# Decoder layer on one Trainium2 core: the router's columns after the second Gram matrix, the expert ranks in larger pieces, the last layer norm by 128 tokens

## The chip, the core and the metric

The kernel runs on one core of a Trainium2 chip. The core has TensorE (PE in the profile, with its weight loads as PEld), VectorE (DVE), ScalarE (ACT), GpSimd (POOL) and SyncE (SP), which here issues all the DMAs. Each engine works through its own instructions in order, and waits on semaphores for the others. The metric is the device time of one execution in microseconds (us).

## The reference

The reference is one decoder layer, on 16 sequences (B) of 512 tokens (S) with 256 channels (C), in float32. There are three sublayers, each followed by a residual sum and a layer norm without gain:

```python
x = layernorm(x + self_attention(x))           # linear: prod over 2 k of (k^T v), no softmax; inner norm, Wo
x = layernorm(x + cross_attention(x, context)) # 16 heads of 64, 64 context tokens a sequence, Wq, Wkv, Wout
x = layernorm(x + mixture_of_experts(x))       # 8 experts, 256 -> 1024 -> 256, relu

# mixture of experts: each expert serves the first `capacity` tokens, in order, with weight > 0
capacity = ceil(b * s / e * 1.0)               # 16*512/8 = 1024
w = softmax(x @ router_w.T + router_b)
out = relu(tokens @ experts_inter[e]) @ experts_out[e] * w
```

Softmax weights are practically never zero. So the expert sublayer serves the first 1024 tokens, that is batches 0 and 1, unless some weight underflows; which tokens are served is nevertheless computed from the weights.

## The kernel before

**Parts.** The linear self-attention is computed from one Gram matrix x^T x of each batch (`gram`, L544: two halves of matmuls, L549 and L554, into one PSUM bank `ps_g`; copies into `g` and `u`; a transpose `ps_gt`, L567). The cross attention first makes keys of the whole context: `context_keys` (L444) transposes the context and the weights (`ps_t`, L233), computes blocks of 128x512 (`ps_kv`, L436, two matmuls each, called kv1, kv2, ... here), copies each into a tile `st` (a pool of two buffers, by DVE or ACT in turn, L188 and L186) and stores it to `k_dram` (L464). The main part of the program then goes through the 16 batches: self-attention, cross attention (`ps_sim` L808, softmax, the transpose into `pT` L798, `ps_x` L828), layer norm, routing. The experts work on the head, batches 0 and 1 (`HEAD_B`, 1024 tokens), in four groups of `TB` = 256 tokens an expert: eight blocks f of `ps_h` (L932, two matmuls each), each with its relu into a tile `hT` by DVE (even f, L940) or ACT (odd f, L938), then `ps_e` (L949), 8 matmuls for each of the two 128-token tiles, and the weighted sum into `x2_head` (L956) on DVE. After the last expert the head is normalised and stored (L960 to L964). The rest of the batches are stored before that, after their own norm (L866); a loop at the end of the program repeats the experts for `n_i` of them, and `n_i` is 0 with these inputs.

**Layer norm.** `normalized` (L252) takes the moments by BN statistics on DVE (L249, L250), makes the reciprocal deviation by Ln and Exp on ACT (L261, L262), yields, then makes the offset `off` on DVE (L265) and applies both on ACT, one instruction for each 128 tokens (L267).

**Router columns.** `router_columns` (L371) turns the router's weights into columns that are appended to other weight matrices, so that router logits come out of later matmuls as 8 more columns (264 = 256 + 8). It has three DVE operations on 8 partitions (L374 to L376), two small transposes (`ps_rw`, L379) and one copy (L380). Its result is read by `router_weights` (L403, about 64 us) and later.

**Ranks.** `ranks` (L869) decides from all the weights which tokens each expert serves: a comparison (L885), two matmuls for sums over tokens (`ps_tot`, L889, and `ps_in`, L891) with their copies (L892, L893), a running sum over 64 token tiles in six doubling rounds (L897, L898), then the ranks, the selected weights `w_sel` and the number of loop rounds `n_i` (L901 to L912). All but the two matmuls is on DVE. It runs after the routing of the last batch.

**Order.** The order of the instructions is written down when the program is built. Six generators, the streams (`grams`, `context`, `self`, `cross`, `routing`, `experts`), issue their instructions piece by piece. `weave` always lets one go on to its next `yield`. A model of engine times (class `Model`, L28) estimates when each piece would end. `yield WAIT` makes a stream ready again only at the modelled end of its last piece, `yield 0.6` in 0.6 us, a plain `yield` at once; among the ready streams that with the smallest planned time (`plan(at, span, total)`) goes next. `beside` starts another stream with its parent's planned time. `in_order` then binds the instructions of PE, DVE, ACT and POOL to this order, so an instruction that waits holds up everything behind it on its engine, also where that is of another stream. SP issues its DMAs in order as well.

Of the kernel before, what the change touches and what calls it, by code (L numbers as in the profile page):

```python
# [9 lines left out]
FP = mybir.dt.float32  # L10
# [8 lines left out]
P = 128  # L19
# [5 lines left out]
WAIT = "wait"  # L25
# [91 lines left out]
def decoder_layer(  # L117
# [25 lines left out]
    nc = tc.nc  # L143

    B, S, C = x.shape
    J = context.shape[1]
    NT = S // P
# [8 lines left out]
    E, _, FF = w_inter.shape  # L156
# [5 lines left out]
    CX = C + E  # L162
    TB = 256
# [52 lines left out]
    x2_head = const.tile([P, HEAD_B, NT, CX], FP, tag="x2_head", name="x2_head")  # L216
# [35 lines left out]
    def normalized(dst, src, NT=NT, mm=None):  # L252


        rstd = small.tile([P, NT], FP, tag="rstd", name="rstd")
        if mm is None:
            mm = moments(NT)
            for t in range(NT):
                moment(mm, t, src(t))
        mv = mm[1]  # L260
        nc.scalar.activation(rstd, mv[:, :, 1], AF.Ln, bias=eps)  # L261
        nc.scalar.activation(rstd, rstd, AF.Exp, scale=-0.5)  # L262
        yield WAIT
        off = small.tile([P, NT], FP, tag="off", name="off")
        nc.vector.scalar_tensor_tensor(off, mv[:, :, 0], -1.0, rstd, ALU.mult, ALU.mult)  # L265
        for t in range(NT):
            nc.scalar.activation(  # L267
                dst[:, t, :], src(t), AF.Identity, bias=off[:, t:t + 1], scale=rstd[:, t:t + 1]
            )


    with ExitStack() as att:
# [17 lines left out]
        wk1 = pool(att, "wk1", 1)  # L290
# [30 lines left out]
        def key_weights():  # L321
# [14 lines left out]
            out=hm, in_=hm, pattern=[[0, NC], [-HD, P // HD], [0, HD]], compare_op=ALU.is_ge,  # L336
# [3 lines left out]
            out=hm, in_=hm, pattern=[[0, NC], [HD, P // HD], [0, HD]], compare_op=ALU.is_ge,  # L340
# [528 lines left out]
        def ranks():  # L869

            place = wk1.tile([P, 7, NTT, E], FP, tag="kq", name="ranks")
            consts = place[:, 6].rearrange("p t e -> p (t e)")
            ones, before = consts[:, :P], consts[:, P:2 * P]
            nc.gpsimd.memset(ones, 1.0)

            nc.gpsimd.affine_select(
                out=before, in_=ones, pattern=[[1, P]], compare_op=ALU.is_gt, fill=0.0,
                base=0, channel_multiplier=-1,  # L880
            )
            pos, tot, cum, nxt, start, rank = (place[:, i] for i in range(6))


            nc.vector.tensor_single_scalar(pos, w_all, FLT_MIN, ALU.is_ge)  # L885
            posf = pos.rearrange("p t e -> p (t e)")
            yield
            ps_tot = bank("ps_tot")
            nc.tensor.matmul(ps_tot, ones, posf, start=True, stop=True)  # L889
            ps_in = bank("ps_in")  # L890
            nc.tensor.matmul(ps_in, before, posf, start=True, stop=True)  # L891
            nc.vector.tensor_copy(tot.rearrange("p t e -> p (t e)"), ps_tot)  # L892
            nc.vector.tensor_copy(rank.rearrange("p t e -> p (t e)"), ps_in)  # L893
            yield
            src, s = tot, 1
            while s < NTT:
                nc.vector.tensor_copy(nxt[:, :s, :], src[:, :s, :])  # L897
                nc.vector.tensor_add(nxt[:, s:, :], src[:, s:, :], src[:, :NTT - s, :])  # L898
                src, nxt, s = nxt, (cum if src is tot else src), s * 2
                yield  # L900
            nc.vector.tensor_sub(start, src, tot)  # L901
            nc.vector.tensor_add(rank, rank, start)
            nc.vector.scalar_tensor_tensor(w_sel, rank, float(CAP), w_all, ALU.is_lt, ALU.mult)
            NB = B - HEAD_B
            least = small.tile([P, NB], FP, tag="least", name="least")
            nc.vector.tensor_reduce(
                least, start.rearrange("p (b t) e -> p b t e", t=NT)[:, HEAD_B:, 0, :], AX.X, ALU.min
            )
            nc.vector.tensor_single_scalar(least, least, float(CAP), ALU.is_lt)
            n_f = small.tile([P, 1], FP, tag="n_f", name="n_f")  # L910
            nc.vector.tensor_reduce(n_f, least, AX.X, ALU.add)
            nc.vector.tensor_copy(n_i, n_f)  # L912
            yield

        def experts():

            wi = wo_ = None
            yield from until(lambda: 0 in head_T and made(head_T[0]))  # L920
            for e in range(E):
                if e == 0:
                    wi = load_inter(e)
                    wo_ = load_outer(e)
                for n in range(CAP // TB):
                    b, t0 = divmod(n * TB // P, NT)
                    yield from until(lambda: b in head_T and made(head_T[b]))
                    hT = []
                    for f in range(NF):
                        ps = bank("ps_h")  # L930
                        for cc in range(NC):
                            nc.tensor.matmul(  # L932
                                ps[:, :TB], wi[:, cc, f * P:(f + 1) * P],
                                head_T[b][:, cc, t0 * P:t0 * P + TB], start=(cc == 0), stop=(cc == NC - 1),
                            )
                        h = ffn.tile([P, TB], FP, tag="hT", name="hT", bufs=12)
                        if f % 2:
                            nc.scalar.activation(h, ps[:, :TB], AF.Relu)  # L938
                        else:
                            nc.vector.tensor_relu(h, ps[:, :TB])  # L940
                        hT.append(h)
                        yield
                    if n == CAP // TB - 1 and e + 1 < E:
                        wi = load_inter(e + 1)
                    yield from until(lambda: finished["routing"] > b)
                    for t in range(TB // P):
                        ps = bank("ps_e")
                        for f in range(NF):
                            nc.tensor.matmul(  # L949
                                ps[:, :C], hT[f][:, t * P:(t + 1) * P], wo_[:, f, :],  # L950
                                start=(f == 0), stop=(f == NF - 1),
                            )
                            if f % 4 == 3:
                                yield
                        acc = x2_head[:, b, t0 + t, :C]
                        nc.vector.scalar_tensor_tensor(  # L956
                            acc, ps[:, :C], w_all[:, b * NT + t0 + t, e:e + 1], acc, ALU.mult, ALU.add
                        )
                    if e == E - 1:
                        y = wk1.tile([P, NT, CX], FP, tag="z", name="y")[:, :TB // P, :C]  # L960
                        yield from normalized(y, lambda t: x2_head[:, b, t0 + t, :C], TB // P)
                        nc.sync.dma_start(
                            out=out[b, t0 * P:t0 * P + TB, :].rearrange("(t p) c -> p t c", p=P), in_=y
                        )  # L964
                    if n == CAP // TB - 1 and e + 1 < E:
                        wo_ = load_outer(e + 1)

# [26 lines left out]
        def beside(st, gen):  # L994

            new = Stream(gen).plan(st.time(), 0.0, 1.0)
            new.ready = model.end
            streams.append(new)
# [44 lines left out]
        def all_grams():  # L1043
            for b in range(B):
                if b >= QB:
                    grams_st.plan(SETUP + (b - QB - 0.8) * STEP, STEP, 2.9)
                yield from until(lambda: finished["states"] > b - 5)
                yield from grams_of([b])
                if b == 0:
                    router_columns(rw)  # L1050
                    yield
                if b == QB - 1:
                    cs.update(rest_of_weights(sp))
                    yield from router_weights(sp)
# [21 lines left out]
        def all_routing():  # L1076
            nonlocal ffn
            for b in range(B):
                routing_st.plan(SETUP + (b + 1) * STEP, STEP, 1.0)
                yield from until(lambda: finished["cross"] > b and ("values", 1) in held)  # L1080
                if b == 0:
                    setup.close()
                    ffn = pool(att, "ffn", 1)
                yield WAIT
                yield from routing(b, done.pop(b)[0])
                finished["routing"] = b + 1
            yield from ranks()

        ffn = None
# [108 lines left out]
```

## Time and profile before

The time is 1398.09 us, the median of three runs (1395.9 to 1403.09). The profiled execution took 1397.24 us.

| what | value |
|---|---|
| profiled execution, own time / its span | 1397.24 / 1395.6 us |
| mean granted clock of TensorE | 0.994 |
| PE idle, 0 to 20 us | 7.5 us (12.49 busy) |
| PE idle, 115 to 1300 us | 6.4 us of 1185 (1178.60 busy) |
| PE idle, 1350 to 1395.6 us | 13.6 us (32.02 busy) |
| granted clock, those three stretches | 0.91, 1.00, 0.91 |
| DMAs `k_dram<-st`, 256 KB: issue to landing | 2.1 to 6.3 us, median by the list of DMAs 4.3 |
| DMAs `out_dram<-y`, 256 KB | median 2.3 us |

These are lines from around the start of the ranks and at the very end, from the timeline. Its columns are start (us), duration (us), engine and source line, operation, output and inputs, shapes, count, and in brackets the idle time before and what ended it.

```profile
1349.81 0.42 DVE L885 TENSOR_SCALAR ranks<-w_all 128x512 f32<-128x512 f32 x1
1350.38 1.10 PE L889 MATMUL ps_tot<-ranks 128*128 128x512 f32 x2
1352.17 7.07 PE L932 MATMUL ps_h<-head_T,wi 128*128 128x256 f32 x32
1388.95 0.37 SPq L962 DMA_DIRECT2D out_dram<-y  x1
```

A matmul instruction of float32 leaves two records in the profile, so the 32 records of `ps_h` are 16 instructions. SPq is the queue of DMA issues: 1388.95 is when the last output was issued.

### The profile page before, as it was taken

How to read it: one execution, taken by the hardware profiler on the slowest of the kernel's cores; microseconds unless marked ns; L12 is line 12 of the kernel's file. 1: busy time of each engine (PE TensorE's matmuls, PEld its weight loads, DVE VectorE, ACT ScalarE, POOL GpSimd, SP SyncE). 2: the span in 40 equal slices, each digit the busy share in tenths (PEclk: the TensorE clock that was granted, in tenths of full speed). 3: DMA queues.
4: the chain of work that ended last, by engine and by line, in shares of the span. 5: the costliest groups of instructions: out<-in, count | busy, mean ns of one | idle time of the engine just before them, and what ended most of it. 6: DMA issues, size and time to landing. Idle time of an engine off the chain costs nothing.

```text
span 1395.6 us, 24180 instructions
## 1 busy us (share of the span) xinstructions
PE 1365.0 (98%) x9630; PEld 1077.3 (77%) x9630; DVE 849.4 (61%) x1953; ACT 399.8 (29%) x904; POOL 203.7 (15%) x140
## 2 busy tenths in 40 slices
PE   7999999999999999999999999999999999999996
PEld 5666676877778787878878787878788877878685
DVE  2355848465674838474665848374756757583842
ACT  1134224132323223141323332231323223332221
POOL 0001112112020112112120211111110202020200
PEclk9999999999999999999999999999999999999998
DMA  8657775502425062513525071515342152506120
GB/s 256 205 136 187 191 197 159 141 32 59 127 74 147 27 149 98 141 62 84 148 59 143 15 186 61 128 59 120 103 104 78 47 153 65 137 16 170 53 62 25
DMA packets 98309, 153.57 MB, mean 110 GB/s; under 512 B 15497, under 2 KB 70033, under 8 KB 98193
## 3 DMA queue, kind: packets, MB, share of 16 engines
q1 hardware_dynamic: 98192, 151.98, 40.0%
q8 instruction: 78, 1.28, 0.4%
q14 instruction: 39, 0.31, 0.1%
HBM read 114.71 MB, written 37.22 MB: 109 GB/s over the span
## 4 chain that ended last, share of the span: by engine, by line
PE 90%; DVE 5%; DMA 2%; ACT 1%; SPq 1%; issue 1%; DVEq 0%; ACTq 0%
PE ps_x L828 16%; PE ps_e L949 15%; PE ps_sim L808 15%; PE ps_h L932 14%; PE ps_gk L623 4%; PE ps_p L705 4%; PE ps_o L681 3%; PE ps_kv L436 3%; PE ps_t L233 2%; PE ps_kq L745 2%; PE ps_vo L486 2%; PE ps_s L635 2%; PE ps_g L549 2%; PE ps_zt L694 1%; PE ps_m L664 1%; PE ps_g L554 1%
## 5 line engine op out<-in xcount | busy, mean ns | idle before, releaser
L932 PE MATMUL ps_h<-head_T,wi 128*128 128x256 f32 x1024 | 238.9, 379 | 0.0
L828 PE MATMUL ps_x<-vo,pT 32*128 32x264 f32 x4096 | 233.1, 383 | 5.7 <-DVE pT L798 3.7
L808 PE MATMUL ps_sim<-kq,x1T 128*128 128x512 f32 x512 | 235.0, 593 | 0.0
L828 PEld LDWEIGHTS ps_x<-vo,pT 32*128 32x128 f32 x4096 | 212.1, 185 | 25.6 <-issue 5.6
L932 PEld LDWEIGHTS ps_h<-head_T,wi 128*128 128x128 f32 x1024 | 193.4, 190 | 38.8 <-issue 12.7
L796 POOL TENSOR_TENSOR s<-s,sm 128x1024 f32<-128x1024 f32 x64 | 121.7, 1901 | 539.7 <-DVE sm L795 501.3
L835 DVE TENSOR_TENSOR x<-ps_x,x 128x264 f32<-128x264 f32 x64 | 23.2, 424 | 224.8 <-PE ps_x L828 224.8
L816 ACT ACTIVATE s<-s 128x512 f32<-128x512 f32 x128 | 80.7, 630 | 276.0 <-DVE s L815 276.0
L808 PEld LDWEIGHTS ps_sim<-kq,x1T 128*128 128x128 f32 x512 | 94.5, 190 | 83.2 <-issue 74.5
L814 DVE TENSOR_REDUCE mx<-ps_sim 128x8 f32<-128x512 f32 x128 | 86.0, 672 | 42.3 <-PE ps_sim L808 41.9
L815 DVE TENSOR_TENSOR s<-ps_sim,mx 128x512 f32<-128x512 f32 x128 | 88.5, 691 | 4.4
L719 POOL TENSOR_TENSOR x<-x,bout 128x1056 f32<-128x1056 f32 x16 | 38.7, 2420 | 319.3 <-ACT hT L938 172.6
L938 ACT ACTIVATE hT<-ps_h 128x256 f32<-128x256 f32 x128 | 46.5, 376 | 133.6 <-PE ps_h L932 133.5
L798 DVE STREAM_TRANSPOSE pT<-s 128x1024 f32<-128x1024 f32 x64 | 78.5, 1227 | 7.0 <-POOL s L796 7.0
L794 DVE TENSOR_REDUCE sm<-s 128x16 f32<-128x1024 f32 x64 | 77.0, 1204 | 0.4 <-ACT s L816 0.4
L695 ACT ACTIVATE zT<-ps_zt,shift,gain 128x512 f32<-128x512 f32 x32 | 23.2, 775 | 188.1 <-PE ps_zt L694 188.1
L267 ACT ACTIVATE x<-x,off,rstd 128x264 f32<-128x264 f32 (+1 forms) x112 | 58.3, 591 | 29.9 <-DVE off L265 29.9
L681 PE MATMUL ps_o<-m,xT 128*128 128x264 f32 x256 | 66.7, 387 | 0.0
L261 ACT ACTIVATE rstd<-bn_mv,eps 128x4 f32<-128x4 f32 (+1 forms) x66 | 19.5, 296 | 163.2 <-DVE bn_mv L250 160.4
L940 DVE TENSOR_SCALAR hT<-ps_h 128x256 f32<-128x256 f32 x128 | 51.7, 408 | 22.2 <-PE ps_h L932 22.1
L705 PE MATMUL ps_p<-wo,zT 128*128 128x264 f32 x256 | 63.1, 387 | 0.0
L436 PE MATMUL ps_kv<-cT,wT 128*128 128x512 f32 x128 | 61.3, 612 | 0.1
(172 smaller groups left out, 1894.6 us busy)
## 6 DMA issues: line engine op xcount, KB each, us to landing
vo<-vo_dram SPq DMA_DIRECT2D x512, 132.0 KB, 4.3
vo_dram<-vst SPq DMA_DIRECT2D x128, 132.0 KB, 2.4
xt<-in_x_dram SPq DMA_DIRECT2D x16, 512.0 KB, 3.9
wi<-L_ffn_experts_inter_dram SPq DMA_DIRECT2D x8, 1024.0 KB, 5.1
gx<-in_x_dram SPq DMA_DIRECT2D x15, 512.0 KB, 5.6
x_rest<-x SPq DMA_DIRECT2D x14, 512.0 KB, 3.2
out_dram<-x SPq DMA_DIRECT2D x14, 512.0 KB, 2.9
k_dram<-st SPq DMA_DIRECT2D x16, 256.0 KB, 4.3
```

The lines of the kernel that those rows point to most:

```text
L436: nc.tensor.matmul(ps, wT[:, cc, r % 4 * P:(r % 4 + 1) * P], cT[:, cc, q * 512:(q + 1) * 512], start=(cc == 0), stop=(cc == NC - 1),)
L681: nc.tensor.matmul(ps[:, :CX], xT[:, cc, t * P:(t + 1) * P], m[:, cc, :], start=(cc == 0), stop=(cc == NC - 1))
L705: nc.tensor.matmul(ps[:, :CX], zT[:, cc, t * P:(t + 1) * P], wo[:, cc, :], start=(cc == 0), stop=(cc == NC - 1))
L796: nc.gpsimd.tensor_mul(s, s, sm.unsqueeze(2).to_broadcast([P, NH, J]))
L798: nc.vector.transpose(probsT[:, :, t, :], s.rearrange("p h (a j) -> p (h a) j", a=2))
L808: nc.tensor.matmul(ps, x1T[:, cc, t * P:(t + 1) * P], kq[:, cc, hf * 512:(hf + 1) * 512], start=(cc == 0), stop=(cc == NC - 1),)
L814: nc.vector.tensor_reduce(mx[:, hs], sim, AX.X, ALU.max)
L815: nc.vector.tensor_sub(s[:, hs, :], sim, mx[:, hs].unsqueeze(2).to_broadcast([P, 8, J]))
L816: nc.scalar.activation(s[:, hs, :], s[:, hs, :], AF.Exp, scale=SCALE)
L828: nc.tensor.matmul(ps[q][:, :CX], probsT[pq, blk].rearrange("p t i -> p (t i)"), vos[c][pq, i, :], start=(c == 0 and i == 0), stop=(c == 7 ...
L932: nc.tensor.matmul(ps[:, :TB], wi[:, cc, f * P:(f + 1) * P], head_T[b][:, cc, t0 * P:t0 * P + TB], start=(cc == 0), stop=(cc == NC - 1),)
L949: nc.tensor.matmul(ps[:, :C], hT[f][:, t * P:(t + 1) * P], wo_[:, f, :], start=(f == 0), stop=(f == NF - 1),)
```

## The change

Three parts. First, `router_columns` is issued after the Gram matrix of batch 1 instead of batch 0. Second, `ranks` gets the smallest planned time of all streams, so that it goes first whenever it is ready, but yields for 0.6 us after each of its pieces; and the doubling rounds yield only after every second one, so that these make three pieces, after s = 4, 16 and 64, with the rest of the function as the last piece. Third, the last layer norm of the head is no longer part of the experts' stream: each 128 tokens get a stream of their own, started as soon as their weighted sum has been issued, with one of two buffers for its output in turn and a DMA of 128 KB instead of one of 256 KB for two tiles.

```diff
@@ ranks() @@
             nc.vector.tensor_single_scalar(pos, w_all, FLT_MIN, ALU.is_ge)
             posf = pos.rearrange("p t e -> p (t e)")
-            yield
+            yield 0.6
             ps_tot = bank("ps_tot")
...
             nc.vector.tensor_copy(rank.rearrange("p t e -> p (t e)"), ps_in)
-            yield
+            yield 0.6
             src, s = tot, 1
             while s < NTT:
                 nc.vector.tensor_copy(nxt[:, :s, :], src[:, :s, :])
                 nc.vector.tensor_add(nxt[:, s:, :], src[:, s:, :], src[:, :NTT - s, :])
                 src, nxt, s = nxt, (cum if src is tot else src), s * 2
-                yield
+                if s in (4, 16, 64):
+                    yield 0.6
...
             nc.vector.tensor_copy(n_i, n_f)
-            yield
+            yield 0.6
+
+        def last_norm(b, t):
+            y = wk1.tile([P, C], FP, tag=("z", "xt")[t % 2], name="y")
+            yield WAIT
+            yield from normalized(y.unsqueeze(1), lambda _: x2_head[:, b, t, :C], 1)
+            yield WAIT
+            nc.sync.dma_start(out=out[b, t * P:(t + 1) * P, :], in_=y)
@@ experts() @@
                         nc.vector.scalar_tensor_tensor(
                             acc, ps[:, :C], w_all[:, b * NT + t0 + t, e:e + 1], acc, ALU.mult, ALU.add
                         )
-                    if e == E - 1:
-                        y = wk1.tile([P, NT, CX], FP, tag="z", name="y")[:, :TB // P, :C]
-                        yield from normalized(y, lambda t: x2_head[:, b, t0 + t, :C], TB // P)
-                        nc.sync.dma_start(
-                            out=out[b, t0 * P:t0 * P + TB, :].rearrange("(t p) c -> p t c", p=P), in_=y
-                        )
+                        if e == E - 1:
+                            beside(experts_st, last_norm(b, t0 + t))
@@ all_grams() @@
-                if b == 0:
+                if b == 1:
                     router_columns(rw)
                     yield
@@ all_routing() @@
                 yield from routing(b, done.pop(b)[0])
                 finished["routing"] = b + 1
+            routing_st.plan(0.0, 1.0, 100.0)
             yield from ranks()
```

## The prediction

> **What bounds the kernel.** I read the page first, for which engine the end hangs on.
>
> ```profile
> PE 1365.0 (98%) x9630; PEld 1077.3 (77%) x9630; DVE 849.4 (61%) x1953; ACT 399.8 (29%) x904; POOL 203.7 (15%) x140
> PE 90%; DVE 5%; DMA 2%; ACT 1%; SPq 1%; issue 1%; DVEq 0%; ACTq 0%
> ```
>
> TensorE (PE) is busy for 1365.0 of 1395.6 us and carries 90% of the chain that ended last. The change leaves its matmuls as they are in number and shape, so only idle time of PE, or time in which PE runs slowly, can move: some 30 us of idling, part of it at the two ends. The list of waits on PE says whose it is (columns: total, times, longest):
>
> ```profile
> PE ps_rw L379 <- DVE early L376: 3.2, 1, 3.2
> PE ps_e L949 <- DVE hT L940: 3.1, 1, 3.1
> PE ps_x L828 <- DVE off L265: 1.9, 1, 1.9
> PE ps_t L233 <- DMA nat<-in_L_xattn_Wkv_dram: 1.0, 1, 1.0
> ```
>
> All four stand in the stretches that the change touches. Then the timeline, to see what is queued around each:
>
> ```profile
> 13.66 0.28 PE L379 MATMUL ps_rw<-ident,early 8*128 8x8 f32 x2 [3.22 <-DVE early L376]
> 14.95 1.97 PE L233 MATMUL ps_t<-ident,nat 128*128 128x128 f32 x8 [1.01 <-DMA nat<-in_L_xattn_Wkv_dram]
> 19.20 7.03 PE L436 MATMUL ps_kv<-cT,wT 128*128 128x512 f32 x16
> ...
> 30.50 1.90 PE L549 MATMUL ps_g<-gx 128*128 128x257 f32 x8
> ...
> 31.93 0.69 DVE L188 COPY st<-ps_kv 128x512 f32<-128x512 f32 x1 [1.59 <-DMA k_dram<-st]
> ...
> 1322.77 14.59 PE L828 MATMUL ps_x<-vo,pT 32*128 32x264 f32 x256 [1.92 <-DVE off L265]
> ...
> 1361.83 1.41 DVE L940 TENSOR_SCALAR hT<-ps_h 128x256 f32<-128x256 f32 x4
> 1362.30 0.70 PE L949 MATMUL ps_e<-wo__10778,hT 128*128 128x256 f32 x2 [3.06 <-DVE hT L940]
> 1363.35 8.27 PE L949 MATMUL ps_e<-wo__10778,hT 128*128 128x256 f32 x30 [0.36 <-ACT hT L938]
> ```
>
> Last, the windows (length, busy of PE, PEld, DVE, ACT, POOL, then the granted clock): after the wait at 1362 PE is busy, but slow.
>
> ```profile
> 16.00:18.00 2.00, 2.00 (x9) 1.73 (x8) 0.69 (x1) 0.58 (x1) 0.00 (x0) 0.50 1.09 374
> ...
> 1362.00:1364.00 2.00, 1.34 (x4) 0.85 (x5) 1.23 (x4) 2.00 (x6) 0.00 (x0) 0.77 0.01 4
> 1364.00:1366.00 2.00, 2.00 (x6) 1.60 (x5) 0.00 (x0) 0.12 (x1) 0.00 (x0) 0.50 0.36 127
> ```
>
> About 1.7 us are missing there (2 us at 0.77, 2 at 0.50, the next 2 at 0.88), and as much at 14 to 20 us (0.70, 0.50, 0.95). A stall of about 3 us is thus paid once more.
>
> **The end of the program.** The built order of the changed kernel shows that PE runs the same instructions, differently woven; a 128x256 matmul costs 0.432 us (7.07 us for 16 in `ps_h`, L932), a feature block f of `ps_h` two of them, 0.86, a token group of `ps_e` 3.45.
>
> *Ahead of the last `ps_x`.* The wait of 1.92 us is really for `pT` (transposed on VectorE, DVE, 1321.50 to 1322.71), late because DVE did the 256-token norm first. The shorter norm streams let the planner put three more f (2.59 us) ahead of it: PE comes at 1320.85+2.59 = 1323.4, `pT` is ready about 1323.0. With a gap of 0.24 at 1337 that goes too: **-2.2**.
>
> *Ranks.* Before, `ps_tot` and `ps_in` follow `ps_e` at once; now three f stand ahead. PE comes at 1350.5-2.2+2.6 = 1350.9; but DVE, with token norms and hT copies before L885, finishes it about 1351.35 by the row durations: **+0.45** (0 to 1.2).
>
> *The wait of 3.06.* Before, the first hT copy sits behind the entire rank chain on DVE, which ends at 1361.84. From 1359.24 to 1371.62 PE takes 12.38 us for two token groups of 6.91: 5.5 lost (3.06, then 0.36 for ScalarE's hT, the rest the clock). Now f0, f2 and f4 are copied between the pieces. What the built order still leaves in one run on DVE, although there is a yield in it, are the last two doublings (1.38) and everything up to `n_i` (1358.92 to 1361.84), 4.3 us, with f6's copy behind it. DVE: `ps_tot` from 1351.35, its copy (L892) 1.13 later, both copies done 1354.0, six doublings 4.47, the end 2.92, two `off` and f4's copy 0.55, f6's 0.35: 1362.3. PE: 1351.35+1.84 (the two rank products)+4.32 (five f)+2.59 (six matmuls of `ps_e`) = 1360.1. A wait of 2.1 takes the place of 5.5: **-3.4**. That the clock holds is a choice. The Trainium skill ("TensorE: Matmul & The Clock Gate", HAM oscillation) says that a fully idle window of about 3.4 us halves the clock, the windows running free, and advises against gaps over about 3 us. By the rule 3.06 us would be too short for a whole window; the rows show 0.50 after it, so the trace decides there; the 1.92 before `ps_x` left 1.00, so 2.1 should as well. If not, +1.7.
>
> *After the last matmul.* One token is normalised instead of two: -0.55 (BN pair, 1385.88 to 1386.43) and -0.54 (half of the 1.09 for y): **-1.1**. The last output DMA is 128 instead of 256 KB. A rule that speaks against splitting: the skill's "DMA: Bandwidth & Descriptors" (Anatomy of one DMA, for the software-generated path) gives a fixed 2.0 us plus bytes/436e3, by which halving saves 0.3. Rows: 256 KB of y lands in a median 2.3, 128 KB quarters of `gx` in 2.2. I take 0.1, inside the 1.1. Four more y DMAs on SP, each some 0.4 of issue, come 3.45 us apart and delay nothing; SP's load of `n_i` now stands ahead of four of them, not three, with `n_i` written some 20 us before the end. Eight pairs of Ln and Exp (0.50) on an ACT that is 29% busy lie under the matmuls.
>
> Tail: -2.2+0.45-3.4-1.1 = **-6.2**.
>
> **The start.** The three DVE operations (12.65 to 13.60), the two transposes (0.28) and the copy move behind `g` of batch 1. Nothing reads the result before 60 us; the move issues no DMA, but shifts PE's order, and with it SP's: `gx` of batch 3 and the first two key stores now come ahead of weights, whose users are later. The first half of batch 1's Gram product (1.90) fills 10.5 to 12.4. PE then still waits for `nat`, which lands at 14.90: about 2.5 us idle instead of 3.22+1.01, so no gain there except what no longer follows. At full clock eight transposes (1.04, row at 9.29) and the other half (1.06, row at 8.39) put `ps_kv` at 17.0 instead of 19.20: 2.2 earlier; with the clock down again, 18.6.
>
> New is what stands before `ps_rw`. DVE's order is ..., copy of kv6 into `st`, L374, L375, L376. That copy has two buffers and waits for the store of kv4, as kv4's waits for kv2's. Before, it ran at 31.93 and nobody on PE waited for it, since PE went on to batch 2's Gram product at 30.50. Now PE's `ps_rw` stands behind it, and batch 2's product behind `ps_rw`. PE arrives 10.4 us of work after `ps_kv` began, at 27.4; DVE comes at 31.93-2.2 = 29.7, +0.69 for the copy, +0.95, +0.28 on PE: the product begins at 31.65, not 30.50: **+1.15**. The stall of 4 us is longer than that of 3.06, so here rule and rows both take the clock: **+1.7**. PE's order from there until the tail is unchanged, so the shift is carried along. Price of the landing from both sides: stores of `k_dram` land in 2.1 to 6.3 us; in my row 4.3 (kv2) and 3.5 (kv4). Both at 2.1 to 2.5 give a stall near 1 us and a start of about **-1.6**; both at 6.3 give +4.8 more. I stay at the rows themselves, which have the same stores amid the same weights.
>
> Start: 1.15+1.7 = **+2.85**. Sum -6.2+2.85 = -3.35: the profiled execution's own 1397.24 (span 1395.6 and 1.64 around it; 0.85 under the median) becomes 1393.9, the median 1398.09 becomes **1394.7**.
>
> **Rivals.**
> A (0.55) is this sum; its own range is 1391.5 to 1397.5.
> B (0.25): the stores land quickly, `ps_rw` stalls about 1 us and the clock stays. For it: less competes with them than at 14 to 18 us. Against: landings of 4.3 and 3.5 in the very place. -6.2-1.6 = -7.8: 1390.3.
> C (0.10), slower: the queue behind kv6's copy takes all. Landings of 6.3 (+2.0 and +2.8), `ps_kv` not before 18.6 (+1.6), 1.15 and 1.7: start +9.2, sum +3.0: 1401.1. It decides once the start loses over 6.2. For it: SP issues these stores earlier, into DMA engines full at 14 to 18 us (share 1.09). Against: 6.3 is the longest of sixteen.
> D (0.10): the change does only part of what it says. The uncut last run on DVE holds f6, and the 2.1 us there cost the clock after all, +1.7: 1396.4.
>
> **How the numbers follow.** About 0.5% (7.0 us) is what a measurement of this kernel can tell from no change. Faster, under 1391.1: two thirds of B, a fifth of A: 0.29, and 0.03 for a tail better than my DVE order: 0.32. Slower, over 1405.1: a third of C and shifts in the middle that I don't see: 0.06. The range from 1388.8 (B with a tail 1.5 better) to 1398.8 (C in part) leaves out about 2 in 10.
>
> **What would show it.** Tail: `ps_x` without its 1.9; `ps_e` waiting about 2 on hT instead of 3.06, clock 1.00 behind it; last matmul to last DMA issue 2.4 instead of 3.5. Start: `ps_rw` near 31 us, waiting about 4 on `early`, with the kv6 copy waiting on a store, and a clock of 0.5 behind it. Wrong I am if `ps_rw` waits under 1.5, or if the transposes of `nat` come well before 14.9.

## The result, and the profile after

| kernel | median of 10 runs (us) | lowest to highest |
|---|---|---|
| before | 1398.24 | 1395.9 to 1403.62 |
| changed | 1392.86 | 1389.93 to 1394.92 |

The ratio is 0.9953, with a 95% interval from 0.9936 to 0.9969: 6.6 us faster, between 4.3 and 9.0. A second series of the changed kernel, beside other runs of before, gave 0.9942 (0.9925 to 0.9960). The forecast was 1394.7 in a range from 1388.8 to 1398.8. The profiled execution took 1391.12 us with a span of 1389.4, which is 6.1 under that of before.

Busy time and the chain that ended last, from the page of the changed kernel:

```profile
PE 1363.8 (98%) x9630; PEld 1075.8 (77%) x9630; DVE 850.5 (61%) x1957; ACT 402.2 (29%) x912; POOL 203.9 (15%) x140
PE 90%; DVE 6%; DMA 2%; ACT 1%; issue 0%; SPq 0%; DVEq 0%; ACTq 0%
```

TensorE has the same 9630 records of matmuls and the same share of the chain, so the difference is again idle time and slow clock. Its waits in the changed kernel (total, times, longest):

```profile
PE ps_rw L379 <- DVE early L376: 3.3, 1, 3.3
PE ps_t L233 <- DMA nat<-in_L_xattn_Wkv_dram: 3.1, 1, 3.1
...
PE ps_e L957 <- DVE hT L948: 1.8, 1, 1.8
...
PE ps_tot L889 <- DVE off L265: 0.4, 1, 0.4
```

The wait of 1.9 at the last `ps_x` is gone, that for hT has gone from 3.1 to 1.8, and the router's transposes wait as long as before, for another reason. The start of the changed kernel in the timeline:

```profile
15.47 1.09 PE L233 MATMUL ps_t<-ident,nat 128*128 128x128 f32 x8 [3.14 <-DMA nat<-in_L_xattn_Wkv_dram]
17.29 8.75 PE L436 MATMUL ps_kv<-cT,wT 128*128 128x512 f32 x20
29.47 0.69 DVE L188 COPY st<-ps_kv 128x512 f32<-128x512 f32 x1 [1.65 <-DMA k_dram<-st]
30.68 0.34 DVE L376 TENSOR_SCALAR early<-early,rs 8x256 f32<-8x256 f32 x1
31.17 0.35 PE L379 MATMUL ps_rw<-ident,early 8*128 8x8 f32 x2 [3.30 <-DVE early L376]
31.45 3.52 PE L549 MATMUL ps_g<-gx 128*128 128x257 f32 x8
```

The keys begin 1.9 us earlier than before (19.20). Then kv6's copy on DVE waits for a store, the router's operations stand behind it, and TensorE behind them. Batch 2's Gram product begins at 31.45 (before: 30.50) and takes 3.52 instead of 1.90. The windows tell why; the number after those of the five engines is the granted clock:

```profile
30.00:32.00 2.00, 0.83 (x3) 0.78 (x4) 1.13 (x5) 0.00 (x0) 0.00 (x0) 0.79 0.94 297
32.00:34.00 2.00, 2.00 (x6) 1.59 (x5) 0.00 (x0) 0.00 (x0) 0.00 (x0) 0.50 0.73 202
```

The end of the changed kernel in the timeline:

```profile
1325.88 14.52 PE L828 MATMUL ps_x<-vo,pT 32*128 32x264 f32 x256
1353.94 1.10 PE L889 MATMUL ps_tot<-ranks 128*128 128x512 f32 x2 [0.39 <-DVE off L265]
1364.01 0.15 DVE L913 CAST n_i<-n_f 128x1 int32<-128x1 f32 x1
1364.08 0.42 DVE L948 TENSOR_SCALAR hT<-ps_h 128x256 f32<-128x256 f32 x1
1364.55 4.58 PE L957 MATMUL ps_e<-wo__10778,hT 128*128 128x256 f32 x20 [1.75 <-DVE hT L948]
1385.57 0.33 SPq L921 DMA_DIRECT2D out_dram<-y  x1
```

One copy of hT (f6) still stands behind the end of the ranks, and TensorE waits for it, but the clock holds in this window and the next (before: 0.77 and 0.50):

```profile
1362.00:1364.00 2.00, 0.80 (x4) 0.37 (x2) 1.88 (x5) 0.00 (x0) 0.00 (x0) 1.00 0.00 0
1364.00:1366.00 2.00, 1.45 (x7) 1.29 (x8) 0.77 (x3) 0.00 (x0) 0.00 (x0) 1.00 0.00 0
```

The two profiled executions, cut at the same points (the middle row is the end of the last `ps_sim`, after which only the tail is left):

| stretch | before | changed | difference | forecast |
|---|---|---|---|---|
| start to end of last `ps_sim` | 1313.1 | 1315.6 | +2.5 | +2.85 |
| from there to the last matmul | 72.4 | 67.4 | -5.0 | -5.15 |
| last matmul to last output's issue | 3.5 | 2.6 | -0.9 | -1.0 |
| last output's issue to the end | 6.6 | 3.9 | -2.7 | -0.1 |
| span | 1395.6 | 1389.4 | -6.1 | -3.4 |

The last row but one was not foreseen. And whether the first is a cost of the change, or belongs to this one execution, a single profile can't tell: the runs of one kernel lie up to 8 us apart. Hence the experiments. Theory: the tail's parts bring the gain, the moved router columns cost about 2.4 us at the start. Rival: the move costs nothing, since what it delays would have been delayed anyway.

### The profile page after: what moved, and what is told of

Read it like the earlier page. It is cut to its first block, busy times and chain, and to the rows that moved or that the text cites. A ratio compares the mean times of both kernels' runs of the same rounds, so it can differ in the third digit from the quotient of the medians.

```text
span 1389.4 us, 24206 instructions
## 1 busy us (share of the span) xinstructions
PE 1363.8 (98%) x9630; PEld 1075.8 (77%) x9630; DVE 850.5 (61%) x1957; ACT 402.2 (29%) x912; POOL 203.9 (15%) x140
## 4 chain that ended last, share of the span: by engine, by line
PE 90%; DVE 6%; DMA 2%; ACT 1%; issue 0%; SPq 0%; DVEq 0%; ACTq 0%
PE ps_x L828 17%; PE ps_sim L808 15%; PE ps_e L957 15%; PE ps_h L940 14%; PE ps_p L705 4%; PE ps_gk L623 4%; PE ps_o L681 3%; PE ps_kv L436 3%; PE ps_t L233 2%; PE ps_vo L486 2%; PE ps_kq L745 2%; PE ps_s L635 2%; PE ps_g L549 2%; PE ps_zt L694 1%; PE ps_m L664 1%; PE ps_g L554 1%
```

## The experiments

All ratios are to the kernel before, run beside it on the same chip; "tail" is the stretch from the end of the last `ps_sim` to the end of the span in the profile.

| kernel | ratio (95% interval) | median us | tail us |
|---|---|---|---|
| before | 1 | 1398.2 to 1401.0 by group | 82.5 |
| changed, second series | 0.9942 (0.9925 to 0.9960) | 1392.86 | 73.7 |
| changed, router behind batch 0 | 0.9939 (0.9923 to 0.9955) | 1392.19 | 73.8 |
| changed, router split | 0.9944 (0.9923 to 0.9965) | 1391.82 | 73.8 |
| changed, ranks cut once more | 0.9940 (0.9925 to 0.9956) | 1392.41 | 71.8 |
| changed, router split and ranks cut | 0.9931 (0.9913 to 0.9950) | 1391.13 | 71.6 |
| changed, ranks in one run | 0.9961 (0.9945 to 0.9977) | 1396.08 | 77.7 |
| before, router behind batch 1 alone | 1.0000 (0.9988 to 1.0013) | 1401.65 | 82.2 |
| before, norm streams alone | 0.9990 (0.9978 to 1.0002) | 1398.97 | 81.0 |
| before, rank pieces alone | 0.9949 (0.9932 to 0.9965) | 1394.59 | 78.9 |
| before, two DMAs for each output | 0.9992 (0.9981 to 1.0003) | 1399.74 | 82.7 |
| changed, three `st` buffers, three `vst` | 1.0091 (1.0074 to 1.0109) | 1412.71 | 73.8 |
| the same, router split and ranks cut | 1.0044 (1.0030 to 1.0058) | 1406.57 | 71.6 |

### The router's place, alone and taken back

```diff
# in the kernel before
-                if b == 0:
+                if b == 1:
                     router_columns(rw)
```

> The kernel before with the router's columns behind batch 1 alone; ranks and norms as before. Theory 1: the start is that of the changed kernel (wait of 3.3 at the router's transposes near 31, slow clock behind it), +1 to +2.4: 1399.2 to 1400.6 against 1398.2 for before. Theory 2: no slow stretch near 54, 1396 to 1398.

Measured: 1.0000 with an interval of 1.8 us to each side. The stall is there, in the timeline of TensorE:

```profile
33.41 0.26 PE L379 MATMUL ps_rw<-ident,early 8*128 8x8 f32 x2 [3.73 <-DVE early L376]
33.60 2.83 PE L549 MATMUL ps_g<-gx 128*128 128x257 f32 x6
```

and so is the slow clock behind it (0.50 from 34 to 36 us), but the time doesn't show it. The reverse edit puts the columns back behind batch 0 in the changed kernel:

> The changed kernel with the router's columns back behind the Gram matrix of batch 0; ranks and last norms stay as changed. Theory 1 (the move costs what the two traces show at the start, +0.95 us at batch 2's Gram product and +2.4 after the slow clock behind the stall; the gain is all in the end): the start is that of the kernel before (a wait of 3.2 on the router's columns near 13 us, batch 2's Gram product at 30.5), and the time is 1 to 2.4 us under the changed kernel's 1392.9: 1390.5 to 1392. Theory 2 (the move is a gain, since the shifted start spares a stretch of slow clock later, near 54 us): 1393.5 to 1396, with that slow stretch back.

Measured: 1392.19, ratio 0.9939 against 0.9942 and 0.9953 of the changed kernel. No difference in either direction; theory 1's 1 to 2.4 us are not to be seen in one, nor theory 2's slower time in the other.

Where the shift goes is seen when the profiles with two `st` buffers and the router in one piece are sorted by the router's place. The first column is the start of `ps_ks` (the small products behind batch 3's Gram matrix), the second that of the first `ps_vo`, the third where in the first 60 us the clock was halved (each number is the start of a stretch of 3.41 us; "2x" two on end):

| router behind | profile | `ps_ks` | `ps_vo` | halved at |
|---|---|---|---|---|
| batch 0 | before | 49.4 | 79.2 | 14.8, 52.4 |
| batch 0 | changed, router behind batch 0 | 52.0 | 81.8 | 2x 14.0, 55.0 |
| batch 0 | norm streams alone | 50.1 | 81.8 | 14.4, 51.9 |
| batch 0 | rank pieces alone | 50.9 | 82.7 | 14.9, 52.4 |
| batch 0 | two DMAs | 52.3 | 82.4 | 2x 14.7 |
| batch 1 | changed | 51.4 | 81.5 | 31.2 |
| batch 1 | changed, second series | 52.7 | 81.0 | 2x 30.4 |
| batch 1 | ranks cut once more | 51.6 | 81.6 | 31.1 |
| batch 1 | ranks in one run | 52.9 | 82.9 | 15.4, 32.5 |
| batch 1 | router alone | 53.8 | 82.1 | 16.7, 33.7 |

The means are 50.9 and 52.5 us at `ps_ks`, but 81.6 and 81.8 at `ps_vo`: the delay of 1.5 us is used up 30 us later. Each group spreads over about 3 us, so the means are rough; the waits are clearer. These are rows of VectorE and TensorE, the first two of the changed kernel with the router behind batch 0, the last two of the changed kernel itself:

```profile
50.94 0.69 DVE L188 COPY st<-ps_kv 128x512 f32<-128x512 f32 x1 [6.70 <-DMA k_dram<-st]
52.04 1.92 PE L579 MATMUL ps_ks<-u,wk 128*128 128x4 f32 x16 [1.55 <-DVE u L564]
...
48.01 0.69 DVE L188 COPY st<-ps_kv 128x512 f32<-128x512 f32 x1 [3.54 <-DMA k_dram<-st]
51.45 1.84 PE L579 MATMUL ps_ks<-u,wk 128*128 128x4 f32 x16
```

Near 50 us a key copy on VectorE waits for a store, in all five profiles behind batch 0 for 6.4 to 7.4 us, in all five behind batch 1 for 3.5 to 3.9. The copies into `u`, which `ps_ks` needs, stand behind it, so `ps_ks` waits 0.4 to 1.7 us (mean 1.2) in the first five and not at all in the others. A delay of some 2.7 us, near the forecast 2.85, thus shrinks to 1.5 at `ps_ks`, since a wait there falls away. The rest goes with the clock: behind batch 0, four of five profiles lose it once more near 52 us (1.7 us each, 1.4 in the mean), behind batch 1 none. That the wait at `ps_ks` is what brings this slow stretch on is argued from its place; the fifth profile has the wait without the stretch.

### The router split

```diff
# in the changed kernel
                 if b == 0:
+                    router_columns(rw)        # its three VectorE operations alone
                 if b == 1:
-                    router_columns(rw)
+                    router_transposes(rw)     # ps_rw and its copy
```

> The changed kernel, with the three VectorE operations of the router's columns left behind batch 0 and the two transposes with their copy behind batch 1's Gram matrix. So TensorE no longer waits for the queue of key copies on VectorE. Theory 1: no wait at the router's transposes, they come near 27.5 us, batch 2's Gram product begins at 28 to 28.5 instead of 31.45 with the clock at 1.00: -3 and -1.4, 1388.5. Theory 2: TensorE then waits elsewhere for the same key stores (a bank of PSUM whose copy hangs on a store) or a slow stretch comes later: 1391 to 1393.

Measured: 1391.82, ratio 0.9944, as theory 2 says. Theory 1's start did come, and was then lost. TensorE and DVE in the timeline:

```profile
27.02 2.01 PE L552 MATMUL ps_g<-gx 128*128 128x257 f32 x8
...
47.61 0.69 DVE L188 COPY st<-ps_kv 128x512 f32<-128x512 f32 x1 [9.09 <-DMA k_dram<-st]
...
48.71 3.30 PE L582 MATMUL ps_ks<-u,wk 128*128 128x4 f32 x16 [3.04 <-DVE u L567]
```

Batch 2's product begins 4.4 us earlier than in the changed kernel. But the copies of keys go through two `st` buffers, and the two stores issued at 39.3 and 40.3 took 8.2 and 7.8 us to land. DVE stood 9.09 us before the next copy, and the copies into `u`, which `ps_ks` needs, stood behind that one. The lead is down to 2.7 us at `ps_ks` and 1.2 at `ps_vo` (80.3), with two halved stretches from 49.0. So the stores of keys, and the slow clock behind the wait for them, take an early lead back.

### Three buffers for the keys, three instead of four for the values

```diff
-            st = sp.tile([P, 512], FP, tag="st", name="st")
+            st = sp.tile([P, 512], FP, tag="st", name="st", bufs=3)
...
-                    vst = sp.tile([P, 2, CX], FP, tag="vst", name="vst", bufs=4)
+                    vst = sp.tile([P, 2, CX], FP, tag="vst", name="vst", bufs=3)
```

The kernel differs from the changed one in two places, and the expectation names only the first: the tiles `vst`, which carry the products `ps_vo` to their stores in `vo_dram`, have three buffers instead of four.

> The changed kernel with three buffers st for the key blocks instead of two, the order of every engine unchanged. Theory 1 (the wait at the router's transposes is that for the store of kv4): kv6's copy need not wait for it, so the wait of 3.3 falls under 1 and batch 2's Gram product begins at 28 to 28.5 without a slow clock behind it. Theory 1a (two buffers also pace TensorE up to 85 us): the lead holds, ps_ks comes at 46 to 48 and the first ps_vo at 77 to 78.5 (51.4 and 81.5 in the changed kernel), ratio 0.003 under the changed kernel's. Theory 1b (what takes an early lead back is how long the loads and stores of that stretch take): ps_ks again waits, ps_vo at 80 to 82, and the time is the changed kernel's.

And with the router split and the ranks cut as below:

> All three together: router's VectorE operations behind batch 0 and transposes behind batch 1, the further yield in the ranks, three buffers st. Theory 1a: ratio to before 0.989 to 0.991. Theory 1b: 0.992 to 0.994, as with two buffers.

Measured: with this edit in the changed kernel `ps_rw` waits 1.8 (not under 1), batch 2's product begins at 28.9 with the clock halved from 29.7 (expected at full clock), `ps_ks` comes at 49.1, later than expected, and `ps_vo` at 77.3. No `vst` is in use before 78 us, so this part belongs to the `st` buffers: the lead holds up to `ps_vo`, as theory 1a has it. This fits the key stores as the limit up to there, though not strictly: that profile has one halved stretch ahead of `ps_vo`, the changed kernel's two have two each, and SP's loads came to stand elsewhere among its stores (the order of TensorE, VectorE, ScalarE and GpSimd is unchanged).

The whole is slower by 0.9%, and by 0.4% with the other two edits. Compared with the second series of the changed kernel, matmul by matmul, TensorE is 2.7 us ahead at 97 us and 17.7 behind at 218. What lies in this stretch are the copies of `ps_vo`. First ScalarE's waits for the stores of `vst` (total, times, longest) with four buffers and with three, then two of its rows with three:

```profile
ACT vst L186 <- DMA vo_dram<-vst: 21.9, 23, 2.6
ACT vst L186 <- DMA vo_dram<-vst: 50.4, 28, 7.7
...
163.02 0.38 ACT L186 COPY vst<-ps_vo 128x264 f32<-128x264 f32 x1 [3.18 <-DMA vo_dram<-vst]
...
192.50 0.38 ACT L186 COPY vst<-ps_vo 128x264 f32<-128x264 f32 x1 [7.71 <-DMA vo_dram<-vst]
```

VectorE's waits for the same stores grow alike, from 18.3 to 44.8 us. The tiles `vst` are filled in groups of four. With three buffers the fourth waits for the store of the first of its own group: the row at 192.50 for a store issued at 188.57, which landed at 192.34. The stores of the tile four places back, which a fourth buffer would have let it take, had been issued by 174.7; the landing that is recorded was at 177.05. The wait is that long because the stores were issued late: SP issued nothing between 174.7 and 187.6, when a load of `gx` came, and they stood behind it (171.5 to 179.8 in the changed kernel's second series). So the missing `vst` buffer explains these waits, and most likely the loss; a run with three `st` and four `vst` buffers is lacking. Theory 1a is borne out for the start, and what it says of the whole was not tested by either run.

### The rank pieces, alone, in one run, and cut once more

The rank part of the change's diff (pieces and `plan`) in the kernel before:

> The kernel before with the ranks in larger pieces and first in planning alone; norm and router as before. Theory 1: two hT copies get between the pieces, two stay behind the ranks' end; TensorE waits about 1.9 instead of 3.06 and keeps its clock: -3.5 against before in the tail. The wait of 1.9 at the last ps_x stays, and so do the 6.5 us from the last output's issue to the end. Rival: the wait only moves to f4 and stays at about 3 with its slow clock: 0 to -0.5.

Measured: 0.9949, -7.1 us (-4.9 to -9.5), in the profile -3.6 for the tail. TensorE waits still less for hT than expected:

```profile
1368.91 3.29 PE L950 MATMUL ps_e<-wo__10778,hT 128*128 128x256 f32 x14 [0.52 <-DVE hT L941]
```

The wait of 1.92 at `ps_x` stayed, and in this profile the clock was halved behind it (at 1329.0), as it was not in that of before. So the two tails hold one halved stretch each, and the -3.6 are the pieces and 0.6 of a shorter close. The median of the runs gains more than the profile shows, whose execution was the slowest of the six; by the means it is 5.7 us. This kernel is also the changed one without norm streams and router move. Its tail is 5.1 us longer than that of the changed kernel, 1.7 of it the halved stretch, but its runs can't be told from those: what the norm streams add to the ranks is to be seen in the profiles alone.

```diff
# in the changed kernel: every `yield 0.6` of ranks() a plain `yield`, one after each doubling round
```

> The changed kernel with the yields of the ranks as before (plain ones, after each doubling round), still first in planning. In the built order the ranks then stand in one run on VectorE ahead of all hT copies but the first. Theory (the pieces, not the early place, take the wait for hT away): the wait is back at 3 or more with a slow window, tail 78 to 80 instead of 73.8, ratio about 0.998. Rival (the last norms and early place do it alone): tail 74 to 75, ratio as the changed kernel's.

Measured: 0.9961, 0.0019 over the second series of the changed kernel, and a tail 4 us longer. The waits on hT are back, 2.6 us and then 0.3 for ScalarE's copy,

```profile
1365.71 0.70 PE L956 MATMUL ps_e<-wo__10778,hT 128*128 128x256 f32 x2 [2.56 <-DVE hT L947]
```

with a halved stretch from 1367.1. So it is the pieces, with their yields of 0.6 us, that take this wait away. All sizes are a little under those expected (3 or more, 78 to 80, 0.998); why was not tried. The two intervals of the ratios overlap, but the runs, side by side on one chip, differ by 2.9 us in their means.

```diff
# in the changed kernel
+            yield 1.5
             nc.vector.tensor_sub(start, src, tot)
```

> The changed kernel with one more yield (1.5 us) ahead of the subtraction in the ranks, so that the hT copy of f6 stands on VectorE ahead of the last part of the ranks. Theory 1 (the 1.75 us that TensorE waits for hT in the experts' product are the queue on VectorE): the wait goes, the clock stays 1.00, 1391.1 (-1.75). Rival: the copies of the weighted sums and the last norms, now behind the ranks' end, are late instead: 1392.5 to 1393.

Measured: the wait goes entirely. The `ps_e` group runs through its 7.07 us, and f6's copy stands ahead of the end of the ranks:

```profile
1360.04 7.07 PE L958 MATMUL ps_e<-wo__10778,hT 128*128 128x256 f32 x32
...
1361.11 0.42 DVE L949 TENSOR_SCALAR hT<-ps_h 128x256 f32<-128x256 f32 x1
...
1364.20 0.15 DVE L914 CAST n_i<-n_f 128x1 int32<-128x1 f32 x1
```

The tail is 2.0 us shorter (71.8); nothing else became late. The runs can't tell it from the changed kernel (0.9940), since 2 us are 0.0014.

### The norm streams alone

`last_norm` and its call, from the change's diff, in the kernel before:

> The kernel before with the last norms as streams of 128 tokens alone; ranks and router as before. In the built order the ranks, without the early planned time, then slip behind all of the last expert's work on VectorE: their six doublings and the end come after the last norm. Theory 1: no wait for hT and none at the last ps_x, TensorE ends about 7.6 us earlier than before, but 7.4 us of ranks stand on VectorE behind it and the cores can close only after n_i: -3 to -6 against before, the closing stretch after TensorE's last matmul 11 to 12 us instead of 10.1. Rival (what follows n_i is short or runs beside the ranks): -9 or more, under the changed kernel.

Measured: 0.9990, and the tail shorter by 1.5 us. Without the early planned time the ranks come last; the timeline of the end:

```profile
1382.50 0.48 DVE L963 SCALAR_TENSOR_TENSOR x_head<-ps_e,w_all,x_head 128x256 f32<-128x256 f32 x1 [1.53 <-PE ps_e L956]
...
1390.83 0.15 DVE L912 CAST n_i<-n_f 128x1 int32<-128x1 f32 x1
...
1391.08 0.60 ACT L267 ACTIVATE y<-x_head,off,rstd 128x256 f32<-128x256 f32 x1 [6.85 <-DVE off L265]
```

TensorE ends 6.2 us earlier after the last `ps_sim` than before (66.2 against 72.4), and the last token's norm then waits 6.85 us for its `off`, queued behind the ranks. The closing stretch is 14.8, not 11 to 12 us: it was overlooked that `off` stands behind the ranks. So without the early place of the ranks the norm streams lose at the end most of what they gain before it.

### The last output

```diff
# in the kernel before
-                        nc.sync.dma_start(out=out[b, t0 * P:t0 * P + TB, :].rearrange(...), in_=y)
+                        for t in range(TB // P):
+                            nc.sync.dma_start(out=out[b, (t0 + t) * P:(t0 + t + 1) * P, :], in_=y[:, t, :])
```

> The kernel before with each 256-token output stored by two DMAs of 128 KB instead of one of 256 KB; nothing else. The question is the 6.6 us from the last issue to the end, which are 3.85 in the changed kernel. Theory 1 (size: the smaller DMA is through before the fetch of instructions[...]): last landing about 2 us after its issue instead of 3.9, -2 to -2.7. Theory 2 (time: the fetch comes 4.6 us after the last matmul, and only an earlier issue avoids it): the second half is caught as the whole was, 0 to -0.7.

Measured: 0.9992 (-2.7 to +0.4 us). The stretch from the last issue to the end is 1.3 us shorter (5.3); the tail as a whole isn't, since it holds one more halved stretch than that of before. What the DMA records of the traces show, in us after the last output's issue (an instruction fetch is a packet of 16 KB on a queue of its own; smaller ones of 8 KB are left out):

| profile | half of the packets done | last packet done | fetch runs | SP goes on | span ends |
|---|---|---|---|---|---|
| before, 256 KB | 1.38 | 3.49 | 1.09 to 2.46 | 3.96 | 6.60 |
| router alone, 256 KB | 1.36 | 3.23 | 1.74 to 2.78 | 3.84 | 6.48 |
| rank pieces alone, 256 KB | 1.37 | 2.93 | 0.91 to 1.90 | 3.40 | 6.03 |
| two DMAs, the second | 0.87 | 2.89 | 1.25 to 2.31 | 3.38 | 5.31 |
| norm streams alone, 128 KB | 1.15 | 2.41 | 0.77 to 1.72 | 2.89 | 5.00 |
| changed, 128 KB | 1.11 | 1.35 | 1.93 to 3.06 | 1.93 | 3.86 |

In the first five the fetch falls among the packets, and some of these end 1.3 to 2.1 us after the half of them is done. They are few: in the profile of before, 29 of 256 end later than 1.75. In the changed kernel the last packet is through at 1.35 before the fetch begins at 1.93, and in the eight other profiles of it and its relatives at 1.34 to 1.36, with the fetch from 1.67 at the earliest. Halving the DMA alone does not do it: the gain of 1.3 us lies between the two theories, and the second half is caught as well, as theory 2 has it. Nor is the fetch tied to the last matmul: it comes 4.3 to 5.3 us behind it in 13 profiles, 10.6 in that of the norm streams alone, where the output is issued late as well and is caught all the same. There one DMA of 128 KB ends at 2.41, where in the changed kernel it ends at 1.35. By these single profiles about half of the change from 3.49 to 1.35 is the size, and half that the fetch is missed. That the fetch is what holds the late packets up is argued from these times, not tried by itself. The rest of the gain, 0.7 us, lies behind the landing (2.64 to 1.93): SP has its other waits behind it by then.

### Both edits on the changed kernel

The split router and the further yield in the ranks, together:

> The changed kernel with the router's three VectorE operations behind batch 0 and its transposes behind batch 1, and the further yield in the ranks ahead of the subtraction. Theory 1: no wait at the router's transposes, none for hT; the end is that of the kernel with the further yield (71.8 us from the last ps_sim to the end, 73.8 in the changed kernel), the start is no gain by more than the spread of the slow stretches: ratio to before 0.992 to 0.994. Rival (the start's 4 us carry through): 0.990 to 0.991.

Measured: 0.9931, a tail of 71.6 with the wait for hT gone, and no gain from the start: as theory 1 has it. VectorE again stands long for a key store (8.50 us), `ps_ks` waits 2.45, and two halved stretches follow from 52.0. It is the lowest ratio of all, but its interval (0.9913 to 0.9950) overlaps those of the changed kernel, so that it beats the changed kernel is not shown.

And the changed kernel itself in its second series:

> The changed kernel itself, beside the kernels of this group. Both theories: ratio to before 0.9935 to 0.997; tail from the last ps_sim to the end 73.8 plus 1.7 for each slow window in it.

Measured: 0.9942 and 73.7.

## Why the prediction was right, and where not

The direction, the range and the likeliest case's own range (1391.5 to 1397.5) held. The gain was about twice the forecast, -6.6 against -3.35. Two terms of the sum were off, the start and the last DMA. With both put right (0 and -2.7) it would be -8.8, at the far end of the interval of the first series (-4.3 to -9.0) and near the middle of that of the second (-5.6 to -10.5).

**The tail's waits: right.** These numbers are of the two profiles. The last `ps_x` lost its 1.92 and the stretch from the last `ps_sim` to the last matmul fell by 5.0 (forecast 5.15). The new wait at `ps_tot` was 0.39 (0.45), the remaining one for hT 1.75 (2.1; the prediction's own times, 1362.3 and 1360.1, make it 2.2), on f6 and behind `n_i` as named, with the clock at 1.00.

**That 2.1 us would leave the clock alone: right here, but for a weak reason.** I argued from the 1.92 before `ps_x`. With the rank pieces alone the same 1.92 did halve the clock. Where the wait falls in the chip's window decides, as shown below.

**After the last matmul: the term that was mis-sized.** The norm brought 0.9 of the 1.0. For the last DMA the sum had 0.1, from medians of 2.3 and 2.2 us for 256 and 128 KB. In the profiles the stretch shrank by 2.7: the landing in the profile before was not the median but 3.95 us (SP goes on at 3.96), a number that could have been read there, since it ended the span. The rule weighed there (the Trainium skill, "DMA: Bandwidth & Descriptors", Anatomy of one DMA, for the software-generated path) was no better: it has 0.3 for the halving. The runs don't show this part by itself: two DMAs alone gave -2.7 to +0.4, norm streams alone 0.9990.

**The start: the mechanism was right, the step after it was wrong.** `ps_rw` stood behind kv6's copy, waited 3.3 (about 4), and the clock fell; batch 2's product came at 31.45 (31.65). The step that failed is "PE's order from there until the tail is unchanged, so the shift is carried along". The runs put the move at 0 with 1.8 us to each side. An equal order does not carry a delay through a stretch that another resource limits: here the key stores, which hold TensorE at `ps_ks` for 1.2 us on average when it comes early, with a slow stretch behind that in four of five profiles. The +2.5 in the two profiles at the last `ps_sim` is 1.7 from one more halved stretch on the way (three against two) and 0.8 of the rest; that it lies so near the forecast 2.85 is chance.

**The rivals.** B's short stall did not come; the gain that it would have brought came from the last DMA instead. C's landings of 6.3 and more do occur with two `st` buffers, at 39 to 44 us, but only where the router's VectorE operations stand behind batch 0; with them behind batch 1 the longest is 5.2. D's clock drop at the hT wait did not occur. (Two thirds of B and a fifth of A are 0.28, not 0.29; nothing hangs on it.)

## What to carry to other kernels

Before a delay is added to the end of a program, ask which resource limits the stretch behind it; a wait taken earlier costs nothing as far as it replaces a later wait on that resource. For the last instructions of a program, the landing of that very DMA in the trace is the number to use, not the median of its kind. A part that needs another (the norm streams, which without the early ranks gave 0.9990) shows little when it is tried alone, so each part needs both tests: alone, and taken out. And a run that gives one tile another buffer has to keep those of all others, or its total says nothing of the first.

## What the runs showed of the hardware

Ahead of the last matmul, the clock record of every profile consists of stretches of 3.41 us at half speed, each worth 1.7 us where TensorE has work. With windows of 3.41 us laid so that these stretches fill whole ones, the 14 profiles hold, from 10 us to the last matmul, 35 full-speed windows in which TensorE was busy for less than 44.5% (a limit drawn from these same data): all 35 were followed by a window at half speed. Of 124 windows between 44.5% and 90% it was 10, of 5415 busier ones 8 (all eight between 67 and 80 us, among transposes and matmuls with 8 columns). The first 10 us are left out: seven windows there, each the first full one of its profile, were 19% to 42% busy and not followed by half speed, and why is open. Behind the start, then, the window need not be idle: a wait of 1.92 us that falls wholly into one halves the clock (rank pieces alone, 44% busy), and one of 3.2 us that is cut by a boundary does not (before, at 335 us, 55% and 50% busy). The rule weighed in the prediction (the Trainium skill, "TensorE: Matmul & The Clock Gate", What's actually happening and HAM oscillation), read there as one fully idle window, asks for more than the chip did here; the measurement decides.

The phase of these windows differs from execution to execution: the twelve profiles with two `st` buffers have two to seven halved stretches ahead of the tail. This makes up much of the spread of the runs. Over three groups of 18 to 27 runs of the kernel before, the time scatters by about 2 us (standard deviation), time multiplied by the granted clock of the run by about 1. It is also part of the gain. In the second series the changed kernel's six runs have a mean granted clock of 0.9948, the 18 of before beside them 0.9921. That is worth 3.8 us, of the 7.9 by which the mean times differ; 1.0 to 1.7 of the 3.8 lie behind the last matmul, where TensorE idles. The rest, 2 to 3 us, is an estimate for one to two halved stretches fewer in a run, where the forecast had one fewer in the tail and one more at the start.
